# One eviction a step and token rows in a ring of groups, in a recommendation kernel on one Trainium2 core

## The chip, the cores and the metric

The kernel runs on one core of one Trainium2 chip. The metric is the device time of one launch in microseconds; lower is better. Engine names are those of the profile: PE is the matmul engine (PEld its weight loads), DVE the vector engine, ACT the scalar engine, POOL the engine that issues the gathers, SP the one that issues the plain loads and stores.

## What is computed

The batch is 16384 rows. Each row has 32 token indices into a table of 50000 x 300 floats, three lists of 20 indices into tables of 1000, 5000 and 10000 rows of 64, and four single indices into tables of 100, 50, 20 and 1000 rows of 64. The reference, cut to what matters:

```python
tok = word_emb[token_idx].mean(axis=1)                  # 300 wide
e1, e2, e3 = (emb_mhK[mhK_idx].mean(axis=1) for K in 1, 2, 3)
o1, o2, o3, o4 = (emb_ohK[ohK_idx] for K in 1, 2, 3, 4)
emb = jnp.concatenate([tok, e1, e2, e3, o1, o2, o3, o4], axis=1)   # 748 wide
wide = sum of the seven one-column tables' entries at the same indices
h = relu(emb @ W1 + b1)      # 1024
h = relu(h @ W2 + b2)        # 512
h = relu(h @ W3 + b3)        # 256
return sigmoid(h @ Wd + bd + wide)
```

## The kernel before, in words

The batch is cut into 128 tiles of 128 rows; four tiles are a block of 512 rows, on which the dense layers run. The instructions stand in an order written out by hand: each engine has one queue and runs it in order, and a wait at its head holds up all that is behind it.

The token table stays in HBM. `tokens` (L206) issues, on POOL, one indirect DMA per token (L212): 128 rows of 300 floats, one for each row of the tile. Two tokens go to one tile `tok_rows`, of which there are six, so that twelve gathers are the most that can be ahead of the additions. When more than `TOK_LAG` = 3 pairs are under way, `add_up` (L197) adds the oldest to the tile's features `g` on DVE: the two rows to each other (L202), the result to `g` (L203); the first pair of a tile goes straight to `g` (L200). A gather into a `tok_rows` buffer waits until DVE has read that buffer.

The small tables live in SBUF as bf16 terms, cut into 138 slices of 128 rows. Their lookups are sums, done with counts: for every batch row, `one_hots` (L280) makes on DVE two one-hot matrices for the 64 lookups, one of the row within a slice (128 wide), one of the slice (138 wide); `counts` multiplies them on PE (L298), which gives how often each table row is looked up, and ACT moves the counts from PSUM to the fp8 tile `cnt` (L305). A later sum, `small_sums` (L323), multiplies `cnt` by the terms on PE, and DVE adds up the three terms (L330).

A tile is worked through in 11 steps of 6 batch rows in each half of the partitions (the last step has 4). A step is, in each engine's order: DVE makes the next step's one-hots (two buffers of each), PE makes this step's counts, ACT evicts them, POOL gets its share of the tile's gathers and DVE its additions, PE does its share of the previous tile's sums, and its share of the previous block's dense layers (L376, with ACT's relu at L385). At a block's end the features of four tiles are transposed on PE (L366) and scaled on DVE (L367). A `Paced` object hands out the shares.

A bank of PSUM holds 512 floats, that is three batch rows of 138 counts. So the 6 rows of a step are two halves: each half is 6 matmuls (3 rows, two partition halves) to a tile `pc` of two banks, and one eviction of 828 elements a partition. There are two such tiles, so a half's matmuls wait for the eviction of the same half of the step before:

```python
for k0 in range(0, rows, PER_BANK):           # PER_BANK = 3
    n = min(PER_BANK, rows - k0)
    pc = ps_c.tile([P, 2, 512], F32, name="pc")
    ...                                        # 2 * n matmuls
    nc.scalar.activation(cnt[...], pc[:, :, 0 : n * n_h], AF.Copy, scale=0.5, saturate=True)
```

Of the kernel before, what the change touches and what calls it, by code (L numbers as in the profile page):

```python
# [8 lines left out]
F32 = mybir.dt.float32  # L9
BF16 = mybir.dt.bfloat16  # L10
FP8 = mybir.dt.float8e3
I32 = mybir.dt.int32
U32 = mybir.dt.uint32
# [6 lines left out]
N_MH, EMB = 20, 64  # L20
ROW = EMB + 1
D1, D2, D3 = 1024, 512, 256
TOK_GROUP = 2
TOK_LAG = 3
BLOCK = 512
HALF = P // 2
N_SMALL = 3 * N_MH + 4
# [17 lines left out]
def kernel(  # L45
# [29 lines left out]
    for f in SMALL:  # L75
        n = -(-tables[f].shape[0] // P)
        slices[f] = (n_h, n_h + n)
        n_h += n
    PER_BANK = 512 // n_h

    tokp = ctx.enter_context(tc.tile_pool(name="tok", bufs=2 * TOK_LAG))
    const = ctx.enter_context(tc.tile_pool(name="const", bufs=1))
    idxp = ctx.enter_context(tc.tile_pool(name="idx", bufs=2))
    keyp = ctx.enter_context(tc.tile_pool(name="keys", bufs=1))
# [4 lines left out]
    wp = ctx.enter_context(tc.tile_pool(name="wide", bufs=2 * NSUB))  # L89
    xp = ctx.enter_context(tc.tile_pool(name="x", bufs=1))  # L90
    ps_h = ctx.enter_context(tc.tile_pool(name="ps_h", bufs=2, space=bass.MemoryType.PSUM))
    ps_c = ctx.enter_context(tc.tile_pool(name="ps_c", bufs=2, space=bass.MemoryType.PSUM))
    ps_g = ctx.enter_context(tc.tile_pool(name="ps_g", bufs=2, space=bass.MemoryType.PSUM))


# [21 lines left out]
    nc.vector.memset(scale[0:EMB, 4:5], 1.0 / N_MH)  # L117


    iota_i = const.tile([P, n_h], I32, name="iota_i")  # L120
    nc.gpsimd.iota(iota_i, pattern=[[1, n_h]], base=0, channel_multiplier=0)
    iota = const.tile([P, n_h], BF16, name="iota")
    nc.vector.tensor_copy(iota, iota_i)
# [68 lines left out]
        for sb, dram in ((wd_sb, wd), (b1_sb, b1), (b2_sb, b2), (b3_sb, b3), (bd_sb, bd)):  # L192
            nc.sync.dma_start(out=sb, in_=dram)

    under_way = []

    def add_up(rows, g, first):  # L197
        a, b, n = rows[:, 0:TOK_D], rows[:, TOK_D : 2 * TOK_D], TOK_D
        if first:
            nc.vector.tensor_add(g[:, 0:n], a, b)  # L200
        else:
            nc.vector.tensor_add(a, a, b)  # L202
            nc.vector.tensor_add(g[:, 0:n], g[:, 0:n], a)  # L203

    def tokens(g, it):


        for q in range(N_TOK // TOK_GROUP):
            rows = tokp.tile([P, TOK_GROUP * TOK_D], F32, name="tok_rows")
            for t in range(TOK_GROUP):  # L210
                j = q * TOK_GROUP + t
                nc.gpsimd.indirect_dma_start(  # L212
                    out=rows[:, t * TOK_D : (t + 1) * TOK_D],
                    out_offset=None,
                    in_=word,
                    in_offset=bass.IndirectOffsetOnAxis(ap=it[:, j : j + 1], axis=0),
                )
            under_way.append((rows, g, q))
            if len(under_way) > TOK_LAG:
                rows, to, old_q = under_way.pop(0)  # L220
                add_up(rows, to, old_q == 0)
            yield 1

    def last_tokens():
        for rows, g, q in under_way:
            add_up(rows, g, q == 0)

    def load_indices(blk):

# [16 lines left out]
    def lookup_keys(ix):  # L246

        pairs = NSUB // 2
        low = keyp.tile([P, pairs, 2, N_SMALL], I32, name="low")
        nc.vector.tensor_single_scalar(low, ix, P - 1, op=ALU.bitwise_and)
        nc.vector.tensor_single_scalar(ix, ix, 7, op=ALU.logical_shift_right)
        keys = keyp.tile([P, pairs, 2, 2 * N_SMALL], BF16, name="keys")
        for r in range(pairs):
            view = keys[:, r].rearrange("p w (f c) -> p w f c", f=2)
            nc.vector.tensor_copy(view[:, 0], low[:, r])
            nc.vector.tensor_add(view[:, 1], ix[:, r], first)
        pk = ps_h.tile([P, pairs, 2, P], BF16, name="pk", tag="ph")  # L260
        for r in range(pairs):
            for w in range(2):
                nc.tensor.transpose(pk[:, r, w, :], keys[:, r, w, :], ident_bf)
        sc = scp.tile([P, pairs, 2, 2, HALF, 2], BF16, name="sc")
        n = pairs * 2 * P
        nc.vector.tensor_copy(
            sc.rearrange("p r w t b d -> p (r w t b) d"),
            pk.rearrange("p r w b -> p (r w b)").unsqueeze(2).to_broadcast([P, n, 2]),
        )
        return sc  # L270
# [17 lines left out]
    def counts(cnt, hot, i):  # L288

        b = i * ONEHOT  # L290
        rows = min(ONEHOT, HALF - b)
        for k0 in range(0, rows, PER_BANK):
            n = min(PER_BANK, rows - k0)
            pc = ps_c.tile([P, 2, 512], F32, name="pc")
            for k in range(n):
                for f in range(2):
                    half = slice(f * HALF, (f + 1) * HALF)
                    nc.tensor.matmul(  # L298
                        pc[:, f, k * n_h : (k + 1) * n_h],
                        hot[0][half, k0 + k, :],  # L300
                        hot[1][half, k0 + k, :],
                        start=True,
                        stop=True,
                    )
            nc.scalar.activation(  # L305
                cnt[:, :, b + k0 : b + k0 + n, :].rearrange("l f k h -> l f (k h)"),
                pc[:, :, 0 : n * n_h],
                AF.Copy,
                scale=0.5,
                saturate=True,  # L310
            )

    def small_sums(g, cnt):


        by_slice = cnt.rearrange("l f p h -> l (f p) h")
        for i in (0, 2, 6, 4):
            pair = SMALL[i : i + 2]
            pg = ps_g.tile([P, 2, 3 * ROW], F32, name="pg")
            for j, f in enumerate(pair):  # L320
                h0, h1 = slices[f]
                for h in range(h0, h1):
                    nc.tensor.matmul(  # L323
                        pg[:, j, :], by_slice[:, :, h], terms[:, h, :], start=(h == h0), stop=(h == h1 - 1)
                    )
                    if h < h1 - 1:
                        yield 1
            at = TOK_D + i * ROW
            n = len(pair)
            nc.vector.tensor_reduce(  # L330
                g[:, at : at + n * ROW].rearrange("p (f d) -> p f d", f=n),
                pg[:, 0:n, :].rearrange("p f (c d) -> p f d c", c=3),
                AX.X,
                ALU.add,
            )
            yield n if i != 6 else n + LULL

    def wide_term(g):
        wide = wp.tile([P, 1], F32, name="wide")
        at = TOK_D + EMB  # L340
        nc.vector.tensor_reduce(
            wide,
            g[:, at : at + 6 * ROW].rearrange("p (c d) -> p c d", d=2 * ROW)[:, :, 0:2],
            AX.XY,
            ALU.add,
        )
        nc.vector.tensor_add(wide, wide, g[:, G_COLS - 1 : G_COLS])
        return wide
# [95 lines left out]
    for t in range(tiles + 1):  # L444
        s = t % NSUB
        sums = None
        if before:
            sums = Paced(small_sums(*before), n_h + LULL, STEPS)
        if t < tiles:
            if s == 0 and t:  # L450
                it, sc = next_it, next_sc
            g = gp.tile([P, G_COLS], F32, name="g")
            cnt = cp.tile([P, 2, HALF, n_h], FP8, name="cnt", tag="counts")
            toks = Paced(tokens(g, it[:, s, :].bitcast(U32)), N_TOK // TOK_GROUP, STEPS)
        else:
            last_tokens()
        for i in range(STEPS):
            if t < tiles:
                hot_now = hot
                if s == 1 and i == 0 and t + NSUB < tiles:  # L460
                    next_it, ix = load_indices(t // NSUB + 1)
                if s == 2 and i == 0 and t + NSUB < tiles + 1:
                    next_sc = lookup_keys(ix)
                if i < STEPS - 1:
                    hot = one_hots(sc, s, i + 1)
                elif t + 1 < tiles:
                    hot = one_hots(next_sc if s == NSUB - 1 else sc, (s + 1) % NSUB, 0)
                counts(cnt, hot_now, i)
                if t == 0 and i % 3:
                    next(tables_on_chip, None)  # L470
                if t == 0 and i == STEPS - 1:
                    load_weights()
                toks.go()
            if sums:
                sums.go()
            if layers:
                layers.go()
        if before:
            sums.finish()
            gs.append(before[0])  # L480
            wides.append(wide_term(before[0]))
        before = (g, cnt) if t < tiles else None
        if t == 0:
            for _ in tables_on_chip:
                pass
        if len(gs) == sizes[0]:
            if layers:
                layers.finish()
            steps = STEPS * (sizes[1] if len(sizes) > 1 else 1)
            layers = Paced(mlp(b0, transposed(gs), wides), mlp_size, steps)  # L490
            b0 += len(gs) * P
            gs, wides, sizes = [], [], sizes[1:]
# [40 lines left out]
```

## Time and profile before

| | |
|---|---|
| median of 14 runs | 7354.14 us (7335.25 to 7371.55) |
| the profiled execution | 7337.11 us, span 7335.3 us |
| PE, busy | 5866.1 us, 80% |
| POOL, busy | 4069.4 us, 55% |
| DVE, busy | 3608.0 us, 49% |
| ACT, busy | 2626.6 us, 36% |
| L212 gathers | 4096, 993 ns each |
| L305 evictions | 2816, 842 ns each |
| L298 count matmuls | 16384, 879.5 us in all, 1045.2 us of idle ahead of them |
| L202, L203, L200 additions | 3968, 464 to 471 ns each |

The profile has the busy time of each engine, groups of instructions by line with the idle time of their engine just before them and what ended it ("releaser"), a list of waits, the chain of work that ended last, and timelines. In groups, "128x828 fp8e3<-128x828 f32" is partitions x elements written and read. Idle time ahead of an instruction costs something only where the engine is on the chain.

### The profile page before, as it was taken

The numbers are of one execution on the slowest core, as the hardware profiler recorded it, in microseconds if no ns is written. First come the engines' busy times: TensorE is split into PE (matmuls) and PEld (weight loads), VectorE is DVE, ScalarE is ACT, GpSimd is POOL, SyncE is SP. The second block draws the span as 40 slices with busy tenths as digits, with TensorE's granted clock in tenths as the row PEclk, the third lists the DMA queues.
The fourth block names the chain that finished last, engine by engine and source line by source line (L and its number), as shares of the span: only waits on it lengthen the run. The fifth ranks groups of instructions, "written<-read, shape, count | busy, mean of one in ns | idle before, by whom it ended". The sixth has DMA issues, their size and how long they took to land.

```text
span 7335.3 us, 103052 instructions
## 1 busy us (share of the span) xinstructions
PE 5866.1 (80%) x41320; PEld 3522.6 (48%) x41320; DVE 3608.0 (49%) x8013; ACT 2626.6 (36%) x3408; POOL 4069.4 (55%) x4103
## 2 busy tenths in 40 slices
PE   3688888888788788888887878887878887878889
PEld 2444444444444444444444444444444444444457
DVE  5545454545444544445444544545445544545443
ACT  4333333333333333333333333333333333333333
POOL 5555555555555555555555555555555555555552
PEclk8789998989888988889888998899899899988899
DMA  5333333333333333333333333333333333333331
GB/s 140 90 89 90 88 87 89 91 91 90 87 89 88 86 92 86 88 88 89 91 88 87 92 88 92 87 91 86 88 89 90 87 88 89 88 91 87 90 86 47
DMA packets 245344, 652.52 MB, mean 89 GB/s; under 512 B 108977, under 2 KB 111988, under 8 KB 244863
## 3 DMA queue, kind: packets, MB, share of 16 engines
q0 software_dynamic: 196608, 629.41, 31.3%
q1 hardware_dynamic: 48255, 16.53, 1.0%
q8 instruction: 323, 5.29, 0.3%
q14 instruction: 158, 1.29, 0.1%
HBM read 645.59 MB, written 0.07 MB: 88 GB/s over the span
## 4 chain that ended last, share of the span: by engine, by line
PE 50%; another core or an unknown queue 25%; ACT 14%; issue 6%; DVE 4%; POOL 1%; DMA 0%; SPq 0%; DVEq 0%; ACTq 0%; POOLq 0%
PE ph L376 23%; PE pg L323 17%; ACT cnt L305 12%; PE pc L298 8%; ACT h L385 1%; PE pt L366 1%; DVE x L367 1%; PE po L399 1%; POOL tok_rows L212 1%; DVE slice L280 0%; DVE g L330 0%; DVE tok_rows L202 0%; DVE g L203 0%; PE po L403 0%
## 5 line engine op out<-in xcount | busy, mean ns | idle before, releaser
L212 POOL DMA_INDIRECT tok_rows<-in_word_emb_dram,it x4096 | 4068.5, 993 | 3186.2 <-DVE g L203 2188.1
L305 ACT ACTIVATE cnt<-pc 128x828 fp8e3<-128x828 f32 (+1 forms) x2816 | 2221.4, 842 | 3372.3 <-remote 1391.8
L323 PE MATMUL pg<-terms,cnt 128*128 128x195 bf16 x17664 | 2143.3, 272 | 268.1 <-issue 254.4
L280 DVE TENSOR_TENSOR row<-iota,sc 128x768 bf16<-128x768 bf16 (+1 forms) x1408 | 765.1, 543 | 2658.3 <-remote 1328.3
L323 PEld LDWEIGHTS <-cnt 128*128 128x128 fp8e3 x17664 | 1769.7, 147 | 491.7 <-issue 353.8
L298 PE MATMUL pc<-slice,row 64*128 64x138 bf16 x16384 | 879.5, 232 | 1045.2 <-ACT cnt L305 886.3
L376 PE MATMUL ph<-x,w_sb 128*128 128x512 f32 (+5 forms) x3264 | 1615.2, 622 | 40.2 <-issue 37.6
L298 PEld LDWEIGHTS <-row 64*128 64x128 bf16 x16384 | 570.2, 97 | 2176.0 <-issue 1642.7
L376 PE MATMUL ph<-h,w_sb 128*128 128x512 f32 (+2 forms) x2720 | 1377.3, 633 | 24.4 <-issue 22.3
L203 DVE TENSOR_TENSOR g<-g,tok_rows 128x300 f32<-128x300 f32 x1920 | 904.6, 471 | 65.6
L202 DVE TENSOR_TENSOR tok_rows<-tok_rows 128x300 f32<-128x300 f32 x1920 | 891.1, 464 | 0.0
L376 PEld LDWEIGHTS ph<-x,w_sb 128*128 128x128 f32 (+1 forms) x3264 | 605.1, 209 | 509.7 <-issue 498.3
L280 DVE TENSOR_TENSOR slice<-iota,sc 128x828 bf16<-128x828 bf16 (+1 forms) x1408 | 803.9, 571 | 0.0
L385 ACT ACTIVATE h<-ph,b_sb 128x512 f32<-128x512 f32 (+2 forms) x476 | 315.3, 662 | 1147.8 <-remote 634.5
L376 PEld LDWEIGHTS ph<-h,w_sb 128*128 128x128 f32 x2720 | 515.2, 213 | 409.1 <-issue 406.8
L330 DVE TENSOR_REDUCE g<-pg 128x130 f32<-128x390 f32 (+1 forms) x512 | 249.8, 509 | 812.4 <-remote 366.8
L367 DVE TENSOR_SCALAR x<-pt,scale 128x512 f32<-128x512 f32 (+4 forms) x204 | 140.8, 717 | 112.6 <-PE pt L366 103.5
L366 PE MATMUL pt<-ident,g 128*128 128x128 f32 (+1 forms) x768 | 123.7, 290 | 52.3 <-DVE x L367 51.8
L366 PEld LDWEIGHTS pt<-ident,g 128*128 128x128 f32 (+1 forms) x768 | 83.5, 142 | 91.8 <-DVE x L367 83.9
L305 ACT ACT_TABLE_LOAD x32 | 41.1, 1283 | 145.8 <-PE pc L298 145.0
L399 PE MATMUL po<-h,wd_sb 128*1 128x512 f32 (+2 forms) x136 | 65.5, 603 | 0.3
L200 DVE TENSOR_TENSOR g<-tok_rows 128x300 f32<-128x300 f32 x128 | 59.2, 463 | 0.0
(32 smaller groups left out, 347.5 us busy)
## 6 DMA issues: line engine op xcount, KB each, us to landing
tok_rows<-in_word_emb_dram,it POOLq DMA_INDIRECT x4096
ix<-in_idx_dram SPq DMA_DIRECT2D x128, 32.0 KB
w_sb<-in_W_dram SPq DMA_DIRECT2D x6, 512.0 KB
it<-in_idx_dram SPq DMA_DIRECT2D x32, 64.0 KB
w_sb<-in_W_dram SPq DMA_DIRECT2D x1, 2048.0 KB
raw<-in_mh_dram SPq DMA_DIRECT2D x1, 975.0 KB
out_dram<-h SPq DMA_DIRECT2D x31, 2.0 KB
raw<-in_mh_dram SPq DMA_DIRECT2D x1, 292.5 KB
```

The costliest lines, as they stand in the source:

```text
L202: nc.vector.tensor_add(a, a, b)
L203: nc.vector.tensor_add(g[:, 0:n], g[:, 0:n], a)
L212: nc.gpsimd.indirect_dma_start(out=rows[:, t * TOK_D : (t + 1) * TOK_D], out_offset=None, in_=word, in_offset=bass.IndirectOffsetOnAxis(ap ...
L280: nc.vector.tensor_tensor(one[:, 0:rows, :].rearrange("p i (n d) -> p i n d", d=2), iota[:, 0:n].rearrange("p (n d) -> p n d", d=2).unsque ...
L298: nc.tensor.matmul(pc[:, f, k * n_h : (k + 1) * n_h], hot[0][half, k0 + k, :], hot[1][half, k0 + k, :], start=True, stop=True,)
L305: nc.scalar.activation(cnt[:, :, b + k0 : b + k0 + n, :].rearrange("l f k h -> l f (k h)"), pc[:, :, 0 : n * n_h], AF.Copy, scale=0.5, sat ...
L323: nc.tensor.matmul(pg[:, j, :], by_slice[:, :, h], terms[:, h, :], start=(h == h0), stop=(h == h1 - 1))
L330: nc.vector.tensor_reduce(g[:, at : at + n * ROW].rearrange("p (f d) -> p f d", f=n), pg[:, 0:n, :].rearrange("p f (c d) -> p f d c", c=3) ...
L366: nc.tensor.transpose(pt[:kk, s * P : (s + 1) * P], chunk(g, k), ident)
L367: nc.vector.tensor_scalar(x[:kk, k, 0:n], pt[:kk, 0:n], scale[:kk, k : k + 1], None, ALU.mult)
L376: nc.tensor.matmul(ph[:, 0:n], weights[:kk, k, m * P : (m + 1) * P], src[:kk, k, 0:n], start=(k == 0), stop=(k == len(kks) - 1),)
L385: nc.scalar.activation(dst[:, m, 0:n], ph[:, 0:n], AF.Relu, bias=bias[:, m : m + 1])
```

## The change

It has two parts. In the first, the counts of a step go to one PSUM tile of four banks (two partition halves x two groups of up to three rows), and one instruction evicts all 1656 elements a partition. There is one such tile, so the next step's counts wait for the whole eviction.

In the second, the twelve token rows stand in one tile `ring` with three groups of five rows each. Four of a group's rows are gathered (`TOK_GROUP` = 4), the first holds the sum so far. One `tensor_reduce` over the five rows (four for the first group of a tile) writes the sum to the first row of the next group, and for a tile's last group to the features. It is issued when the next group's gathers have been (`TOK_LAG` = 1). The features tile `g` is allocated one tile later than before, and `iota_i` shares a buffer with `low`. A tile has 8 groups, handed out over 11 steps.

```diff
-TOK_GROUP = 2
-TOK_LAG = 3
+TOK_GROUP = 4
+TOK_LAG = 1
+TOK_RING = 3
...
-    tokp = ctx.enter_context(tc.tile_pool(name="tok", bufs=2 * TOK_LAG))
+    tokp = ctx.enter_context(tc.tile_pool(name="tok", bufs=1))
...
-    ps_c = ctx.enter_context(tc.tile_pool(name="ps_c", bufs=2, space=bass.MemoryType.PSUM))
+    ps_c = ctx.enter_context(tc.tile_pool(name="ps_c", bufs=1, space=bass.MemoryType.PSUM))
...
-    iota_i = const.tile([P, n_h], I32, name="iota_i")
+    iota_i = keyp.tile([P, n_h], I32, name="iota_i", tag="low")
...
+    GROUP_ROWS = 1 + TOK_GROUP
+    ring = tokp.tile([P, TOK_RING * GROUP_ROWS, TOK_D], F32, name="ring")
+    n_groups = N_TOK // TOK_GROUP
     under_way = []
-
-    def add_up(rows, g, first):
-        a, b, n = rows[:, 0:TOK_D], rows[:, TOK_D : 2 * TOK_D], TOK_D
-        if first:
-            nc.vector.tensor_add(g[:, 0:n], a, b)
-        else:
-            nc.vector.tensor_add(a, a, b)
-            nc.vector.tensor_add(g[:, 0:n], g[:, 0:n], a)
-
-    def tokens(g, it):
-
-
-        for q in range(N_TOK // TOK_GROUP):
-            rows = tokp.tile([P, TOK_GROUP * TOK_D], F32, name="tok_rows")
-            for t in range(TOK_GROUP):
-                j = q * TOK_GROUP + t
+    features = {}
+
+    def add_up(t, q):
+
+        n = t * n_groups + q
+        row, next_row = (k % TOK_RING * GROUP_ROWS for k in (n, n + 1))
+        to = features[t][:, 0:TOK_D] if q == n_groups - 1 else ring[:, next_row, :]
+        rows = ring[:, row + (q == 0) : row + GROUP_ROWS, :]
+        nc.vector.tensor_reduce(to, rows.rearrange("p t d -> p d t"), AX.X, ALU.add)
+
+    def tokens(t, it):
+
+
+        for q in range(n_groups):
+            row = 1 + (t * n_groups + q) % TOK_RING * GROUP_ROWS
+            for r in range(TOK_GROUP):
+                j = q * TOK_GROUP + r
                 nc.gpsimd.indirect_dma_start(
-                    out=rows[:, t * TOK_D : (t + 1) * TOK_D],
+                    out=ring[:, row + r, :],
...
-            under_way.append((rows, g, q))
+            under_way.append((t, q))
             if len(under_way) > TOK_LAG:
-                rows, to, old_q = under_way.pop(0)
-                add_up(rows, to, old_q == 0)
+                add_up(*under_way.pop(0))
             yield 1
...
-        for k0 in range(0, rows, PER_BANK):
-            n = min(PER_BANK, rows - k0)
-            pc = ps_c.tile([P, 2, 512], F32, name="pc")
-            for k in range(n):
-                for f in range(2):
-                    half = slice(f * HALF, (f + 1) * HALF)
-                    nc.tensor.matmul(
-                        pc[:, f, k * n_h : (k + 1) * n_h],
...
-            nc.scalar.activation(
-                cnt[:, :, b + k0 : b + k0 + n, :].rearrange("l f k h -> l f (k h)"),
-                pc[:, :, 0 : n * n_h],
...
+        n = rows // 2
+        pc = ps_c.tile([P, 2, 2, 512], F32, name="pc")
+        for k in range(rows):
+            for f in range(2):
+                half = slice(f * HALF, (f + 1) * HALF)
+                at = k % n * n_h
+                nc.tensor.matmul(
+                    pc[:, f, k // n, at : at + n_h],
...
+        nc.scalar.activation(
+            cnt[:, :, b : b + rows, :].rearrange("l f (g k) h -> l f g (k h)", g=2),
+            pc[:, :, :, 0 : n * n_h],
...
         if before:
-            sums = Paced(small_sums(*before), n_h + LULL, STEPS)
+            features[t - 1] = g = gp.tile([P, G_COLS], F32, name="g")
+            sums = Paced(small_sums(g, before), n_h + LULL, STEPS)
...
-            toks = Paced(tokens(g, it[:, s, :].bitcast(U32)), N_TOK // TOK_GROUP, STEPS)
+            toks = Paced(tokens(t, it[:, s, :].bitcast(U32)), n_groups, STEPS)
```

## The prediction

> **What bounds the kernel now.** I read the page's busy shares first, then the waits, then one stretch of the timeline. No engine is full: PE 80%, POOL 55%, DVE 49%, ACT 36%. The chain of waits therefore matters more than any one busy figure:
>
> ```profile
> PE 50%; another core or an unknown queue 25%; ACT 14%; issue 6%; DVE 4%; POOL 1%; DMA 0%; SPq 0%; DVEq 0%; ACTq 0%; POOLq 0%
> ```
>
> A quarter of the span (1840 us) is on the chain as "unknown". The list of waits says who stands there:
>
> ```profile
> POOL tok_rows L212 <- DVE g L203: 2188.1, 1050, 10.5
> ...
> ACT cnt L305 <- remote: 1391.8, 363, 10.6
> ACT cnt L305 <- PE pc L298: 1336.2, 615, 6.4
> DVE row L280 <- remote: 1328.3, 245, 9.6
> ...
> PE pc L298 <- ACT cnt L305: 886.3, 628, 8.1
> ```
>
> The columns are the total in us, the times and the longest; "remote" is a wait whose releaser the profile could not name. ACT and DVE wait for count matmuls that are long done; PE then waits for ACT, and POOL for DVE. One case from the timelines of ACT, DVE and PE (start, length, what, idle time before):
>
> ```profile
> 2996.04 0.69 ACT L385 ACTIVATE h<-ph,b_sb 128x512 f32<-128x512 f32 x1 [3.98 <-remote]
> 2998.81 0.86 ACT L305 ACTIVATE cnt<-pc 128x828 fp8e3<-128x828 f32 x1 [2.09 <-remote]
> 3001.64 2.36 ACT L305 ACTIVATE cnt<-pc 128x828 fp8e3<-128x828 f32 x3 [1.97 <-remote]
> ...
> 3001.64 0.43 DVE L280 TENSOR_TENSOR row<-iota,sc 128x512 bf16<-128x512 bf16 x1 [7.94 <-remote]
> ...
> 2993.63 0.54 PE L298 MATMUL pc<-slice,row 64*128 64x138 bf16 x12
> 2994.11 1.34 PE L323 MATMUL pg<-terms,cnt 128*128 128x195 bf16 x13
> 2995.29 1.90 PE L376 MATMUL ph<-h,w_sb 128*128 128x512 f32 x4
> 2999.73 0.36 PE L298 MATMUL pc<-slice,row 64*128 64x138 bf16 x6 [2.54 <-ACT cnt L305]
> 3002.55 0.53 PE L298 MATMUL pc<-slice,row 64*128 64x138 bf16 x6 [2.46 <-ACT cnt L305]
> ```
>
> The 12 count matmuls end at 2994.17. The first half's eviction starts at 2998.81 and the second half's at 3001.64, when DVE too gets the same news. PE's semaphore events in the trace were at 2998.79 and 3001.62: the signals came late, one after the other. Over the run, 1591 of PE's 3907 updates come more than 0.3 us after the latest matmul that could have made them; of those of ACT and DVE, three do. It depends on the gathers. Counting how many gathers POOL had issued without a break when the matmul ended, the mean delay is 0.09 us with none, 0.2 to 0.3 with one to three, 0.8 with four, 1.5 with five and 3.3 to 3.9 with six to eight. In the stretch above POOL issues nine in a row, 1.25 us apart, and the last signal comes when they have landed.
>
> So a tile is a cycle: steps of 3.5 us (620 of 1407 steps are under 3.8 us) while the stream of gathers is young, then a long one; 530 exceed 5 us, mean 7.5. The mean step is 5.16 us. The work would allow 3.5; POOL's 32 gathers at 1.25 us need 40 us of a tile's 57, so if the stalls go, POOL is the next to be late.
>
> **What the Trainium skill says.** "TensorE: Matmul & The Clock Gate", The cost: per-tile semaphore tail, prices an increment at about 26 ns. That holds here only without gathers. The same page, Why this matters for your kernels, says that PE idle for over some 3 us drops to a lower clock; the trace agrees, with a granted clock of 0.53 over 3002.50 to 3008.35, and four L376 matmuls taking 3.43 us there against 1.90. "VectorE: DVE Perf Modes", The perf-mode tier table (the rule you actually need), gives tensor_reduce a 1x mode alone. "SBUF — State Buffer", Who interferes with whom, says that a DVE instruction with two SBUF inputs contends with GpSimd's reads and tensor_reduce does not; gathers are 946 ns in the median and 993 in the mean, so this can give POOL at most 47 ns x 4096, or 190 us, of time that isn't its bound.
>
> **The change, part by part.** Sums are against the profiled execution, 7337.1 us (span 7335.3); the median of the 14 runs is 7354.1, or 17 more.
>
> *Counts: one tile, one signal, one eviction.* ACT first. The forms 128x828 at 862 ns and 128x276 at 410 give 0.82 ns an element and 184 ns fixed, so 1656 elements take 1.54 us against the pair's 1.61. This saves 0.07 us x 1408, about 100 us of an engine that is 36% busy: nothing. In a quiet step all of it lies under PE's other work: counts 0.5, then 3.0 of L323 and L376, while the eviction is done 1.6 us after the counts. If a signal is over 1.4 us late, that cover is gone.
>
> Signals: PE makes 4085 updates, 2816 of them for the counts. They become 1408, so all fall by 34%. From the events, the second half's eviction starts over 0.3 us later than the first half's eviction and its own matmuls allow in 250 steps, together 328 us. A single signal takes the first one's turn, so that goes: between 0 and -328, and I take 0.8 of it, **-262**, since PE's waits ahead of the second half sum to 367 (of the 1045 us of idle on L298). Other signals, of relu (634 us "remote" on L385) and of the sums (367 on L330), have fewer ahead of them: 0 to -300; I take 6% of the 1001, **-60**. The slow clock after a long wait goes with some of the waits: 2.3 us in the case above; 0 to -250, I take **-75**, some 33 such restarts.
>
> Against it stands the lost overlap. Before, six matmuls run while ACT empties the other half, and with one four-bank buffer all twelve wait for the whole eviction. From signal to last count matmul it was 1.61 + 0.05 + 0.36 = 2.02 us and becomes 1.54 + 0.05 + 0.54 = 2.13; with the slow clock 2.19 becomes 2.65. That is +0.1 to +0.46 in the 431 steps where PE waited ahead of the second half; I take 0.25, **+107**, with +43 to +200 as bounds. Queued behind the waiting count matmuls on PE are the sums and the layers, and ACT's relu and DVE's L330 and L367 wait for these.
>
> *Token rows.* DVE loses 15 pairs of additions (464 + 471 ns) and one addition a tile, 14.5 us, and gains seven reduces of 1500 elements and one of 1200. The trace has no such reduce from SBUF. The nearest, L330, takes 561 ns for 390 elements and 351 for 195: 1.08 ns an element and 141 ns fixed. So 1500 take 1.76 us, or 1.7 by the one-element rate of the additions (467 ns for 300 with 155 fixed, as in L280's two forms); a tile takes 13.4 to 13.8, and DVE gains about 1 us a tile, 90 to 150 us. DVE's token lines are under 1% of the chain each: 0 to -70, I take **-20**. If strided rows were read at half rate, DVE would need 26 us a tile and still fit in 57, though it then delays the next one-hots by 3.3 us instead of 1.9: up to +300 for that.
>
> POOL: 4096 gathers of the same rows remain, and twelve rows in flight remain (6 x 2, now 3 x 4). What moves is the step in which room comes free: four rows at a time, in steps 0, 1, 2, 4, 5, 6, 8 and 9 of eleven, where two or four came free in every step. A reduce waits until the last of four rows has landed, and behind it in DVE's queue wait the next one-hots. A gather takes up to 2.6 us to land, so POOL must be six rows ahead at that moment; at the steps' starts it is seven to twelve ahead. That wait I price at 0, with +150 as bound. The index queue on SP, the moved g tile and the shared buffer of iota cost nothing: first or rare uses, all under the steps.
>
> Sum: -262 - 60 - 75 + 107 - 20 = **-310**, so 7027 in such an execution and 7045 beside the median.
>
> **Rivals.**
> 1. *Slower: bursts of four feed the blockade.* When signals stop, POOL goes on until the freed rows are used up. If the new quantum leaves one row more at that moment, each of about three long waits a tile lasts 1.25 us longer: 3 x 128 x 1.25 = +480, and with the clock and refills above at -190 net it ends near 7640; it decides from about half a row on average. For: room comes in fours, and the delay grows from the fourth gather on. Against: the total is twelve rows as before, and steps 3, 7 and 10 free none.
> 2. *Much faster: the signals keep up.* Late signals in a row follow each other at multiples of 0.7 us, commonly 0.7 to 2.9. Before, 2.9 are wanted a step, after 1.9; at some 2 us each a step of 4 us could go on under a full stream. One of three long waits a tile (6 us) gone is 128 x 6, -770, about 6580.
> 3. *No difference.* If both halves' signals come together when the gathers have landed, as 600 of 1020 successive late pairs do within 0.2 us, merging saves only what the lost overlap costs: 7340 to 7368.
>
> **Numbers.** My forecast 0.42, rival 2 0.16, rival 1 (with a slow reduce) 0.35, rival 3 0.07. Under 0.2% this kernel's measurement can't tell a change from none. Faster 0.58, same 0.07, slower 0.35. The range is 6600 to 7620; my forecast's own is 6850 to 7300.
>
> **What would show it.** Right: L305 at 1408 instructions of about 1.5 us; "ACT cnt <- remote" and "DVE row <- remote" down by over a fifth; PE's wait for ACT under 800 us; POOL's gathers and their 946 ns as before; reduces near 1.7 us. Wrong: PE's wait for ACT above 1100 us with POOL's unbroken streams longer (rival 1), a reduce near 3 us, or DVE waiting for gathers to land.

## The result and the profile after

The changed kernel takes 7814.1 us (median of 10 runs, 7717.2 to 7882.8), the kernel before 7355.0 us (47 runs): ratio 1.0586, 95% interval 1.0568 to 1.0605. The ratio leaves out the runs that are over 1.5% above the fastest of their kernel, so it lies below the 1.062 of the two medians. The forecast was 7045, with 7620 as its upper end.

All counted work is as the change says: 1408 evictions, 1024 reduces, 4096 gathers. From the page after, the chain and three groups (busy us, mean ns of one | idle time of the engine ahead of it):

```profile
PE 47%; another core or an unknown queue 27%; ACT 9%; issue 7%; DVE 7%; POOL 2%; DMA 0%; DVEq 0%; ACTq 0%; POOLq 0%
...
L218 POOL DMA_INDIRECT ring<-in_word_emb_dram,it x4096 | 4073.6, 995 | 3648.6 <-DVE ring L209 1537.3
L310 ACT ACTIVATE cnt<-pc 128x1656 fp8e3<-128x1656 f32 (+1 forms) x1408 | 2124.1, 1509 | 4158.8 <-remote 2456.5
L209 DVE TENSOR_REDUCE ring<-ring 128x300 f32<-128x1500 f32 (+1 forms) x896 | 2503.3, 2794 | 1.4 <-issue 0.9
...
L303 PE MATMUL pc<-slice,row 64*128 64x138 bf16 x16384 | 834.4, 239 | 1410.9 <-ACT cnt L310 1188.2
```

PE is as busy as before (5862 us against 5866); the span grew by 474 us, and PE's idle time by 366 us at the counts (1045 to 1411) and by 106 at the sums (268 to 374). DVE, with 1.4 us of idle time ahead of its reduces, does not wait for rows. From the list of waits (total us, times, longest):

```profile
ACT cnt L310 <- remote: 2456.5, 398, 14.3
...
DVE row L285 <- remote: 1971.1, 310, 12.0
POOL ring L218 <- DVE ring L209: 1537.3, 283, 10.9
ACT cnt L310 <- PE pc L303: 1316.8, 702, 9.0
PE pc L303 <- ACT cnt L310: 1188.2, 321, 10.5
```

These are the waits of before under new line numbers, and all can last longer. PE's wait for ACT came 628 times before, 8.1 us at the longest, and now comes 321 times, 10.5 at the longest; the two "remote" waits came 363 and 245 times before and now come 398 and 310 times. Six of the seven longest pieces of the chain are now "unknown" ones of 14 us. Here is one of them, from the timeline of all engines (start, length, what, idle time ahead and its releaser):

```profile
3272.93 2.94 DVE L209 TENSOR_REDUCE ring<-ring 128x300 f32<-128x1500 f32 x1
...
3277.14 1.55 ACT L310 ACTIVATE cnt<-pc 128x1656 fp8e3<-128x1656 f32 x1 [1.56 <-remote]
...
3278.11 2.88 DVE L209 TENSOR_REDUCE ring<-ring 128x300 f32<-128x1500 f32 x1
3278.74 0.55 PE L303 MATMUL pc<-slice,row 64*128 64x138 bf16 x12 [1.75 <-ACT cnt L310]
...
3279.32 0.95 POOL L218 DMA_INDIRECT ring<-in_word_emb_dram,it  x1 [0.30 <-issue]
...
3289.34 0.95 POOL L218 DMA_INDIRECT ring<-in_word_emb_dram,it  x1 [0.30 <-issue]
3292.82 1.55 ACT L310 ACTIVATE cnt<-pc 128x1656 fp8e3<-128x1656 f32 x1 [14.13 <-remote]
3292.82 0.56 DVE L285 TENSOR_TENSOR row<-iota,sc 128x768 bf16<-128x768 bf16 x1 [11.83 <-remote]
...
3294.42 0.87 PE L303 MATMUL pc<-slice,row 64*128 64x138 bf16 x12 [7.98 <-ACT cnt L310]
```

The counts are done at 3279.29. DVE's reduces, two of which are shown, have set rows free four at a time, and POOL starts nine more gathers, from 3279.32 to 3289.34, without a break. Their last packet ends at 3291.85. Only after that, 2.5 us after the last gather is issued, does PE's signal get through, to ACT and DVE at once, 13.5 us late.

Over the run: I took the steps whose (last) eviction starts more than 4 us after its matmuls, and counted the gathers started in between. Before there are 312 such steps, 3.6 gathers each; after, 274 with 4.6. Steps over 10 us went from 36 (388 us together) to 170 (2042 us). A second profile of the kernel before, taken later, has 3.9 gathers and 19 such steps, so a difference of 0.3 gathers between two profiles means nothing.

### The profile page after: what moved, and what is told of

It reads as the page before. It is cut to its first block, busy times and chain, and to the rows that moved or that the text cites. A ratio compares the mean times of both kernels' runs of the same rounds, so it can differ in the third digit from the quotient of the medians.

```text
span 7809.6 us, 98189 instructions
## 1 busy us (share of the span) xinstructions
PE 5862.1 (75%) x41320; PEld 3567.8 (46%) x41320; DVE 4687.1 (60%) x5069; ACT 2554.1 (33%) x2000; POOL 4074.5 (52%) x4103
## 4 chain that ended last, share of the span: by engine, by line
PE 47%; another core or an unknown queue 27%; ACT 9%; issue 7%; DVE 7%; POOL 2%; DMA 0%; DVEq 0%; ACTq 0%; POOLq 0%
PE ph L381 20%; PE pg L328 16%; ACT cnt L310 8%; PE pc L303 8%; DVE ring L209 3%; POOL ring L218 2%; PE pt L371 1%; ACT h L390 1%; DVE slice L285 1%; PE po L404 1%; DVE x L372 1%; DVE g L335 1%; DVE row L285 1%; DVE g L209 1%
## 5 line engine op out<-in xcount | busy, mean ns | idle before, releaser
L218 POOL DMA_INDIRECT ring<-in_word_emb_dram,it x4096 | 4073.6, 995 | 3648.6 <-DVE ring L209 1537.3
L310 ACT ACTIVATE cnt<-pc 128x1656 fp8e3<-128x1656 f32 (+1 forms) x1408 | 2124.1, 1509 | 4158.8 <-remote 2456.5
L209 DVE TENSOR_REDUCE ring<-ring 128x300 f32<-128x1500 f32 (+1 forms) x896 | 2503.3, 2794 | 1.4 <-issue 0.9
L328 PE MATMUL pg<-terms,cnt 128*128 128x195 bf16 x17664 | 2181.0, 275 | 374.3 <-issue 306.9
L328 PEld LDWEIGHTS <-cnt 128*128 128x128 fp8e3 x17664 | 1790.2, 147 | 625.5 <-issue 487.9
L303 PE MATMUL pc<-slice,row 64*128 64x138 bf16 x16384 | 834.4, 239 | 1410.9 <-ACT cnt L310 1188.2
L303 PEld LDWEIGHTS <-row 64*128 64x128 bf16 x16384 | 589.2, 101 | 2462.1 <-issue 2105.5
L381 PE MATMUL ph<-h,w_sb 128*128 128x512 f32 (+2 forms) x2720 | 1357.1, 625 | 28.8 <-issue 26.5
L209 DVE TENSOR_REDUCE g<-ring 128x300 f32<-128x1500 f32 x128 | 370.0, 2891 | 0.0
L271 DVE COPY sc<-pk 128x1024 bf16<-128x1024 bf16 x32 | 39.2, 1225 | 19.5 <-PE pk L268 11.4
```

The costliest lines, as they stand in the source:

```text
L209: nc.vector.tensor_reduce(to, rows.rearrange("p t d -> p d t"), AX.X, ALU.add)
L218: nc.gpsimd.indirect_dma_start(out=ring[:, row + r, :], out_offset=None, in_=word, in_offset=bass.IndirectOffsetOnAxis(ap=it[:, j : j + 1] ...
L303: nc.tensor.matmul(pc[:, f, k // n, at : at + n_h], hot[0][half, k, :], hot[1][half, k, :], start=True, stop=True,)
L310: nc.scalar.activation(cnt[:, :, b : b + rows, :].rearrange("l f (g k) h -> l f g (k h)", g=2), pc[:, :, :, 0 : n * n_h], AF.Copy, scale=0 ...
L328: nc.tensor.matmul(pg[:, j, :], by_slice[:, :, h], terms[:, h, :], start=(h == h0), stop=(h == h1 - 1))
L381: nc.tensor.matmul(ph[:, 0:n], weights[:kk, k, m * P : (m + 1) * P], src[:kk, k, 0:n], start=(k == 0), stop=(k == len(kks) - 1),)
```

## The experiments

A piece is the number of rows that come free at once: two before, four after. I held three theories: R, the reduce's price (it takes 2.88 us, not 1.7); Q, the piece; M, the single count tile. L was kept beside Q: the shorter lag or the sum handed along the ring. The lag is how many rows the additions stay behind the gathers: six before, four after. Each run was timed beside the kernel before on its own chip. The table gives the ratio to it, with the 95% interval. The chips differ: the kernel before took 7210 to 7361 us where PE's signals come late under gathers, and 5522 to 5527 us on two others. There two updates in all are late in each profile taken with gathers, but the kernel before itself was not profiled there. A ratio is to be read with its chip.

| | late signals | prompt signals |
|---|---|---|
| changed kernel | 1.059 (1.057 to 1.061) | 1.024 (1.022 to 1.025) |
| first part alone | 0.998 (0.997 to 1.000) | |
| second part alone | 1.055 (1.053 to 1.057) | |
| changed, additions for reduce | 1.060 (1.058 to 1.062) | |
| changed, reduce over neighbours | 1.064 (1.062 to 1.066) | |
| changed, lag of two | | 1.031 (1.029 to 1.034) |
| changed, pieces of two, ten rows | 1.011 (1.007 to 1.015) | |
| before, single rows | | 0.997 (0.996 to 0.998) and 0.998 |
| before, eight rows in flight | | 1.011 (1.009 to 1.012) |
| single rows, one count tile | 0.976 (0.972 to 0.979) | 0.997 (0.996 to 0.998) |
| before, pauses | 0.951 (0.947 to 0.954) | |
| single rows, one tile, pauses | | 1.234 (1.232 to 1.237) |

**The two parts apart.** The first part alone:

```diff
-    ps_c ... bufs=2        # two tiles of two banks, two evictions a step
+    ps_c ... bufs=1        # one tile of four banks, one eviction
```

> The first part alone: one four-bank count tile, one eviction, one signal a step; token rows as before. Theory R (the reduce takes 2.88 us instead of 1.7, and that is the cost): this kernel has no such reduce, so 7100 to 7360 us, PE's wait for ACT under 1045. Theory Q (rows come free in fours, with a lag of one group): the same, 7100 to 7360. Theory M (one count tile in place of two holds PE up): 7500 to 7800, PE's wait for ACT above 1300.

It took 7353.1 us against 7360.6, within 0.2%. The second part alone, with the old counts:

> The second part alone: ring and reduce, counts in two halves as before. R and Q: the whole loss is here, 7750 to 8050, and if merging the counts helps then above the 7814 of the full change. M: 7330 to 7450.

It took 7761.6 us, 401 more than the kernel before, where the whole change cost 459. The loss is in the token part, so M falls, and with it the gain that the prediction had put on the merge. With rows in fours the merge does not help either: the second part alone is below the 7814 of both parts. In the first part's waits (total us, times, longest)

```profile
DVE row L279 <- remote: 1937.4, 344, 9.6
ACT cnt L304 <- remote: 1900.2, 375, 10.0
...
PE pc L297 <- ACT cnt L304: 1211.9, 429, 8.4
```

each of the three is larger than before (1328, 1392, 886). Yet PE's updates (matmuls that raise the semaphore, a counter that other engines wait for) fell from 4085 to 2677, and the sum of their lateness from 3978 to 2949 us. PE's waits at the counts over 5 us went from 15 to 96, and its idle time there from 1045 to 1303 us.

**The reduce's price.** Two ways to give back the predicted 1.7 us, everything else as changed (the first cut to what it does to `ring`'s rows, where a group has its sum so far in row 0):

```diff
-        nc.vector.tensor_reduce(to, rows.rearrange("p t d -> p d t"), AX.X, ALU.add)
+        ring[1:3] += ring[3:5]; ring[1] += ring[2]; to = ring[0] + ring[1]   # first way, three additions
+        near = rows.rearrange("p t d -> p (t d)").rearrange("p (d t) -> p d t", d=TOK_D)
+        nc.vector.tensor_reduce(to, near, AX.X, ALU.add)                     # second way, other elements
```

> The full change, but a group is added up by one addition of 600 elements and two of 300 (about 0.78 + 0.94 = 1.7 us) instead of the 2.88 us reduce; the ring of three groups of four, the lag and the counts stay. R: 7000 to 7400. Q or M: 7650 to 7850, as the changed kernel.

> The full change with the reduce's five inputs taken next to each other instead of 1200 bytes apart, so the sums are over other elements than the reference's; counts of instructions, signals and gathers are those of the changed kernel. If the distance makes the reduce slow, L209 falls from 2.88 to about 1.7 us, and then R says 7000 to 7400, Q and M 7650 to 7850. If a reduce from SBUF costs two cycles an element anyway, L209 stays at 2.9 us and the time at 7750 to 7850.

They took 7804.1 and 7828.3 us. The neighbours' reduce is at the predicted price, in groups by form:

```profile
L210 DVE TENSOR_REDUCE ring<-ring 128x300 f32<-128x1500 f32 x768 | 1311.2, 1707 | 2.3 <-DMA ring<-in_word_emb_dram,it 2.3
```

So 1200 bytes between inputs took it from 1707 to 2884 ns, and giving back the difference, some 1165 us of DVE over the run, did not make the kernel faster: 1.060 and 1.064 beside 1.059. R falls for these chips.

**Where signals are prompt.** The next runs were on such chips.

> The kernel before with groups of one row: twelve single rows in flight (as 6 x 2 before and 3 x 4 after), one addition of 300 a row, room free one row at a time. Theory Q (the size of the piece in which room comes free sets how long the gathers run on without a break, and so how late PE's signals are): bursts shorter than 7.4 gathers and 7050 to 7300 us. Theory L (what cost was the shorter lag or the order of the shares, not the piece): 7300 to 7450, since lag in rows and rows in flight are those of before.

> The full change with TOK_LAG = 2 instead of 1: a group is added up one group later in the order, eight rows behind the gathers instead of four; groups of four and three of them stay. Q: 7700 to 7950, as the changed kernel. L: at least halfway back, 7350 to 7600.

> The kernel before with TOK_LAG = 2, so four pairs, eight rows in flight instead of twelve; piece and order of the shares stay. If a long wait lasts until POOL has used up the room it has (theory Q's mechanism), less room ends it sooner: bursts under 6 gathers and 6700 to 7250 us. If the rows' latency was what the twelve covered, DVE waits for landings and it is 7450 to 7900.

> The changed kernel itself, beside the kernel before, to place it on whichever chip this is. Where the kernel before takes about 7355 us (PE's signals late while gathers run): ratio 1.055 to 1.062 again. Where it takes about 5520 us (signals prompt): theory Q says that without late signals the piece matters only through DVE's waits for landings and the two steps in which nothing comes free, ratio 1.02 to 1.05; theory R (2.88 us reduce) adds DVE time there, 1.04 to 1.08.

Single rows gave 5504.9 us, the lag of two 5699.2, eight rows 5577.1, the changed kernel 5651.5. The longer lag gives nothing back, and eight rows in flight are slower than twelve. DVE waits 1486 us for rows to land with eight; that the twelve cover more of it is likely but not shown, as the kernel before was not profiled there. The changed kernel's 1.024 lies in Q's range (1.02 to 1.05) and below R's (1.04 to 1.08). Of the single rows' 4096 gathers, 3994 ran in one unbroken stream, with two late updates. For these chips the forecasts about late signals test nothing. The changed kernel's waits there are others:

```profile
ACT cnt L310 <- PE pc L303: 2226.1, 1145, 10.5
POOL ring L218 <- issue: 1051.0, 3450, 0.3
...
DVE ring L209 <- DMA ring<-in_word_emb_dram,it: 656.8, 580, 4.2
```

POOL issues nearly all the time (4096 gathers at 1.31 us are 5370 of 5624 us), and DVE waits for landings; PE's signals are not what holds anything up. What of the 2.4% is the piece and what the reduce was not taken apart. A repeat of the single rows, and single rows with one count tile:

> The kernel before with groups of one row, twelve in flight. With late signals (before at 7355 us): Q 7050 to 7300 us with bursts shorter than 7.4 gathers; L 7300 to 7450. With prompt signals (before at 5520 us): 0.997 again.

> Single rows, and counts in one four-bank tile. With late signals: Q and a merge that costs nothing give the time of the single rows alone within 1%, 7000 to 7300 us. With prompt signals: 5480 to 5560 us.

They took 5508.7 and 5509.2 us against 5526.8.

**Without gathers.** First on a chip with prompt signals, before and after:

> The kernel before without its 4096 gathers; the additions stay, over one fixed tile of zeros, so the token part of the features is left out. If gathers are what delays PE's signals: hardly an update over 0.3 us late, steps near 3.5 us, PE's wait for ACT under 100 us, and 5000 to 5400 us in all. If something else delays them (the signals' own number): late updates remain and the time is above 6300.

> The changed kernel without its 4096 gathers; the reduces stay, over a ring of zeros, so the token part of the features is left out. The same kernel before took 5250 us. If what the changed kernel loses needs gathers: 5220 to 5290 us. If the one count tile or the 2.88 us reduce costs by itself: 5350 or more.

They took 5249.7 and 5283.8 us (one run each): without gathers, little of the changed kernel's loss is left there. Later on a chip with late signals:

> The kernel before without its 4096 gathers and with the additions over a fixed tile of zeros, so the token part of the features is left out; it took 5250 us on the chip with prompt signals. If it is the gathers that make the signals late where they are late: hardly an update over 0.3 us late and 5230 to 5300 us there too. If that chip is slow in itself: late updates without gathers, and above 6000.

It took 5246.0 us (one run) beside 7210.8 with gathers, and two updates are late. PE's wait for ACT, 838 to 886 us in the kernel before with gathers, is all but gone from its waits:

```profile
ACT cnt L299 <- PE pc L292: 1804.7, 1157, 8.8
...
PE pc L292 <- ACT cnt L299: 25.3, 9, 8.6
```

So gathers make the signals late there, and without them nothing is left of the difference between the chips (5246 and 5250).

**The piece or the lag.** The changed kernel with three constants changed, and the kernel before for its profile:

```diff
-TOK_GROUP = 4
-TOK_LAG = 1
-TOK_RING = 3
+TOK_GROUP = 2
+TOK_LAG = 2
+TOK_RING = 5
```

> The full change with three constants changed: groups of two, five of them, lag of two groups, so the lag is four rows as in the change, the ring has its fifteen rows (ten gathered, five for sums), and a reduce adds three rows (about 1.9 us at the change's 2.1 ns an element). With late signals (before at 7355 us): Q 7250 to 7550 us and bursts under 8.5 gathers; L (the lag of four rows, or the sum handed from group to group, is what costs) 7650 to 7900. With prompt signals (before at 5520 us): ratio 1.00 to 1.02 by Q, 1.02 to 1.04 by L.

> The kernel before, for its profile on the chip of these runs. If PE's signals are prompt here: fewer than 50 updates over 0.3 us late, POOL's gathers in streams of over 50, steps near 3.9 us, span about 5520 us. If late: the profile shown before the change, about 7340 us.

Signals were late: 7309.7 us against 7230.0 (the profile of the kernel before: 7241.3). Ring, reduce and a lag of four rows stay, and the 5.9% is 1.1%, so L falls. Gathers started in late steps fell from 4.6 to 3.9, as in the second profile of the kernel before, which was taken beside it; steps over 10 us fell from 170 to 60. Two things go with the piece: ten rows are in flight instead of twelve, and the groups are handed out in each of the eleven steps instead of eight of them. A part may be due to these. The remaining 1.1% is not explained. Then one count tile as in the first part, with single rows:

> Counts in one tile and token rows one by one, twelve in flight; only the piece differs from the run of the first part alone (twos, ratio 0.998). With late signals: Q (a piece of one leaves POOL less room when the signals stop: under 3.6 gathers started between a late step's last count matmul and its eviction, against 3.8 with twos and 4.4 to 4.6 with fours) ratio 0.96 to 0.99; if the piece matters only from four on, 0.99 to 1.01. With prompt signals: 0.997 again.

It took 7025.9 us against 7210.8, and 3.3 gathers started in late steps (the first part alone, with twos: 3.8). The same three waits as there are each shorter in total:

```profile
DVE row L280 <- remote: 1538.6, 332, 10.3
ACT cnt L305 <- remote: 1536.0, 355, 8.7
...
PE pc L298 <- ACT cnt L305: 1042.5, 409, 8.4
```

On chips with late signals and with one count tile in all cases, then: one row 0.976, two 0.998, four 1.060 (additions) or 1.059 (reduce). The sum of the lateness of PE's updates has the same order: 2541 us, 2949 (2728 in the ring of twos), and 3226 with fours and the reduce. The mean unbroken stream of gathers, on which Q's first forecasts rested, does not: 7.6 gathers with one row, 6.6 with two, 9.6 with four, and 7.4 in the kernel before. So what holds of Q is that the piece sets how much POOL still starts once the signals have stopped, not that smaller pieces always shorten the streams.

**Bounded streams.** On POOL, in the kernel before:

```diff
+            if q % 4 == 3:
+                for _ in range(5):
+                    nc.gpsimd.memset(scratch, 0.0)      # 128x512, 525 ns each
             under_way.append((rows, g, q))
```

> The kernel before, with five memsets of 512 elements on POOL ahead of every eighth gather pair's group end (after each eight gathers, about 2.5 us), so that no stream of gathers is longer than eight. With late signals: if the unbroken stream is what makes them late, ratio 0.90 to 0.98; if the pauses only take POOL's time (10 us a tile), 1.00 to 1.04. With prompt signals, where POOL's gathers run without a break, the pauses can only cost: 1.10 to 1.20.

It took 6850.3 us against 7210.8. No stream is longer than eight, late steps have 1.8 gathers started in them, and lateness in all is 2494 us (3821 in the second profile of the kernel before). From its chain and its waits:

```profile
issue 24%; POOL 23%; DMA 23%; DVE 19%; PE 9%; ACT 1%; another core or an unknown queue 1%; DVEq 0%; POOLq 0%; SPq 0%; ACTq 0%
...
DVE tok_rows L203 <- DMA tok_rows<-in_word_emb_dram,it: 2385.7, 1439, 6.1
...
ACT cnt L309 <- remote: 936.8, 282, 7.1
```

The "unknown" part of the chain, which was 25% in the kernel before (19% in its second profile), is 1%: updates are still late, but they no longer set the time. ACT's wait for signals is down to 937 us (1301 in the second profile), and DVE now waits for rows, which the pauses hold back. POOL was given 1344 us of extra work (2560 x 525 ns) and the kernel is 5% faster: on these chips the unbroken stream is a cause. The pauses have their price where signals are prompt. They were next put into the single rows with one count tile:

> Single rows, counts in one tile, and five memsets of 512 elements on POOL before the end of every eighth gather. With late signals: shorter streams and less room add up in part, ratio 0.92 to 0.96 (single rows and one tile gave 0.976, pauses 0.951); if both act on the same late signals alone, no better than 0.951. With prompt signals the pauses only cost POOL's time, 1.10 to 1.20.

It took 6826.0 us against 5526.6, more than the 1.10 to 1.20 expected. That is near the 6850 of the pauses on the late chip, and its chain, with two late updates in all, shows why:

```profile
by line: DMA tok_rows<-in_word_emb_dram,it 36.3%; issue 13.5%; POOL scratch L221 11.4%; POOL tok_rows L213 11.3%; DVE g L204 9.4%; DVE row L284 3.6%; PE ph L380 3.0%; DVE slice L284 2.8%; DVE g L334 1.7%; PE pg L327 1.3%; PE pt L370 1.2%; D
```

The pauses and the rows they hold back are the bound, at prompt signals. Whether both remedies add up on a late chip stays open. Of the versions timed on both kinds of chip, single rows with one count tile is the one that beat both kernels on both, by 2.4% and by 0.3% against the kernel before. Single rows with two count tiles were not timed where signals are late, so what the merge adds to them there is open.

## Why the prediction was wrong

Its reading of the bound held: PE's signals come late under unbroken streams of gathers, and PE waits for ACT. One reading was loose: the clock fell at 3001.2, in the second of two idle stretches of PE of 2.5 us with 0.4 us of work between them, so no single one was over 3 us. Rival 1, which had 0.35, is what happened in mechanism. Its rate of 480 us for one more row a late step, times 1.06 rows (3.58 to 4.64), gives +509 where +459 was measured, but that nearness is luck in part: it reckons with three long waits a tile, where there were 2.4 before and 2.1 after, and from the second profile of the kernel before it is 0.7 rows, not 1.06. The steps:

1. **The merge, -262 - 60 - 75 + 107 = -290, measured -7.** This step failed. Signals did fall by the 34% and their lateness by 1029 us, but the term against it was mis-sized. I priced the lost overlap as the refill after a wait, 0.25 us a step, +107 in all. PE's idle time at the counts rose by 258 us instead: with one tile, a late signal stops all twelve matmuls, and waits over 5 us became 96 from 15. That the two effects cancel is what the totals show; no run took one without the other. Rival 1's 7640 counts on the merge too, at -190, which the terms do not give; without that it stands at 7834.
2. **The room, 0, measured +401 by itself.** This step failed too, and it is the larger. "What moves is the step in which room comes free" was priced as DVE's wait for landings, which is 1.4 us. What counts is what POOL may still issue when the signals stop. I had held against the rival that twelve rows stay twelve and that steps 3, 7 and 10 free none. But of the 170 steps over 10 us, 87 are steps 3 and 6, just after three frees in a row and at the last of three; 51 of them are step 3, which frees none itself.
3. **The reduce, 1.7 us, measured 2.88.** L330's rate from PSUM did not carry over to rows 1200 bytes apart in SBUF. But this price was not the miss: at 1.71 us the kernel is no faster, so of the +300 allowed for a half-rate reduce nothing came.
4. **ACT's 1.54 us and "nothing"** held (1.55 for the large form). So did POOL's gathers (995 against 993 ns). The 190 us that I had allowed POOL for a reduce in place of additions, from the Trainium skill's "SBUF — State Buffer", Who interferes with whom, did not come: in the ring they take 982 ns beside additions.
5. The range ended at 7620, just below rival 1's own 7640, though that rival had 0.35.

## What to carry to other kernels

Where a producer runs ahead on freed buffers, look at what it can still do once the consumer has stopped, not only at how many buffers there are: where signals were late, the same twelve rows cost 6% more in pieces of four and, with single rows, 2% less than in pieces of two. Before crediting a merge with fewer signals, ask what work the separate halves let start early. A count of gathers started during each long wait told fours (4.3 to 4.6) from twos (3.6 to 3.9) and ones (3.3), where the busy shares did not. And time a change on more than one chip: here the same change cost 6% on one and 2.4% on another.

## What the runs showed of the hardware

- One program took 7210 to 7361 us on some chips and 5522 to 5527 us on others. The lateness of PE's semaphore updates under gathers goes with it, and without gathers nothing of it is left: 5246 and 5250 us. Where signals are prompt, an update comes 0.02 us after its matmul in the median, through a stream of 3994 gathers too. The gathers' own packets take the same on both (184 ns in the median). Why chips differ stays open.
- DVE's and ACT's updates are not late in the same stretches (3 of them against 1591 of PE's). Late PE updates in a row come together or at multiples of 0.7 us: between them 0.7, 1.4, 2.1 and 2.8 us stand out. Why is not known.
- tensor_reduce over 1500 floats in SBUF took 2884 ns with its inputs 1200 bytes apart and 1707 ns side by side.
